# Taking layer 2's edge columns before the normalization instead of after it, and adding both with one operation

## The chip, the cores and the metric

The kernel runs on one core of a Trainium2 chip. The metric is the device time of one execution in microseconds (us), the median over the runs. The engines are named as in the profile: PE is TensorE's matmul, PEld its weight load, DVE is VectorE, ACT is ScalarE, POOL is GpSimd, SP is SyncE, which issues most DMAs. Each engine works through its own instructions in order.

## The reference

Input x is 16 images of 64 channels and 128x128 pixels, float32. Four layers follow one another, each x = x + f(gn(x)), where gn is a group normalization over 32 groups of two channels.

- Layer 0: f builds the 64x64 Gram matrix of an image's channels and multiplies the image by it, then by a 64x64 matrix.
- Layer 1: f is the sum of the absolute values of two fixed 3x3 derivative filters per channel.
- Layer 2: the first 16 channels are shifted one column to the left, the next 16 one column to the right (zeros come in), and a 3x3 convolution with 64 output channels and a bias follows.
- Layer 3: a 3x3 convolution with weights -1, 0, 1, a 1x1 convolution, a batch normalization over all images, a leaky ReLU and a clip.

## The kernel before

Everything works on 128 partitions: 64 channels times two halves (halves of the image or the two row parities). An image is cut into NS = 8 chunks. Four stages are pipelined over images and chunks: `Gram` (layer 0's matrix), `Front` (layers 0 and 1), `Layer2` and `Layer3` (up to the batch normalization's sums). What is left of layer 3 needs sums over all images; it is a last part that loads two tensors, combines them and stores the output.

**The order is written out by hand.** An outer loop goes over steps, each step over four quarters q = 0, 1, 2, 3. In a quarter, the stages are called in the order Layer3, Layer2, Front, then Gram, and within a stage the images in rising order. One image has its eight chunks i = 0 to 7 in eight successive steps, and stages run a few steps ahead (`first`) and behind (`last`): at the step in which image b-1 is at i = 7 in `Layer2`, image b is at i = -1. Additional calls named "first of 3", "last of 0" and "last of 3" put single operations at the front or the end of a quarter. The wrapper `InOrder` keeps each engine's instructions in the order in which the program makes them, so that this order is what every engine works through. Short chains of tiny operations for statistics (`coefficients`, `gram_chain`) advance by one link per quarter.

**Layer 2, chunk by chunk.** For chunk c of an image:

- `load(c)` is called at i = c-2, q = 1. SP issues 6 DMAs (12 for chunk 7) that bring layer 1's result, channels already shifted, into a tile `v2` of 9 rows of 128 and one more element at each end (128x1154); `whole` is all of the tile, `v` its 9x128 middle.
- At i = c-1, q = 1, ACT normalizes the whole tile in place (`v<-v,co` in the profile, 128x1154). Then POOL makes the edge columns: four `tensor_scalar_mul` of 64x8 each (`edges<-v,co`), one for each side and each half of the partitions. They pick the elements that the shift pushed over the edge out of the normalized tile, multiplied by 1/r (r is gn's factor) where the channel is a left-shifted or a right-shifted one, else by zero. After them, two more POOL operations (`v<-v,kc`, 128x9, "keep") set the columns that the shift has to leave zero.
- At the end of that step ("last of 3"), DVE takes the difference of row parities (`d<-v`) and `twin(1)` has POOL issue two DMAs that copy it to the other half (`qd<-d`). At i = c, q = 0, a second difference is taken, and `twin(0)` has POOL issue two more.
- At i = c, q = 2 and 3, PE multiplies, in shared (`one<-v,wi`) and own products (`two<-d,wi`, `two<-d,w`, `two<-qd,pk`), into PSUM tiles `one` and `two`. At the front of q = 3 ACT moves `one` to SBUF with the bias (`c<-one,co`). `one` has a single buffer, so layer 3's first product of the next chunk (`one<-v,w`) waits for this `c`.
- At i = c+1, q = 0, DVE adds the two edge columns to PSUM's `two` with two operations of 128x8 (`two<-two,edges`), then makes the result x3 with its row sum (`x<-two,c`, 128x1024).

**Around it.** DVE's order in a step is: layer 1's first two operations (`u<-xh`, `e<-xh`), the edge columns and `x<-two,c`, the difference `d<-v`, four operations of layer 1 (`u<-u`, `e<-e`, `u<-u`, `e<-e`), layer 3's `y<-two,c`, then more differences and layer 1's last operations. ACT's order is: layer 3's `c<-one,b_sb` and normalizations `v<-x,co`, layer 2's `v<-v,co`, a copy for Gram (`xw<-xr`), layer 1's two absolute values (`u<-u`, `e<-e`, which need DVE's second pair), a square `junk<-x`, normalizations `xh<-po`, layer 2's `c<-one,co`, and so on. Buffers that matter: `v2` has 3, `edges` 3, PSUM's `one` 1.

The coefficients of layer 2 are a tile of six columns (`co2`): r, -mean*r, 1/r, 1/r masked for left, 1/r masked for right, mean plus bias.

Of the kernel before, what the change touches and what calls it, by code (L numbers as in the profile page):

```python
# [10 lines left out]
F32 = mybir.dt.float32  # L11
AF = mybir.ActivationFunctionType
ALU = mybir.AluOpType
AX = mybir.AxisListType

B, C, H, W = 16, 64, 128, 128
P = 128
# [3 lines left out]
R = 8  # L21
NS = HH // R
# [86 lines left out]
def tile_kernel(ctx: ExitStack, tc: tile.TileContext, x, cw_h, w2_t, b2, wbin_t, w1_t, b1, gamma, beta, consts, out):  # L109
    nc = tc.nc  # L110
    pe, dve, act, sp, pool = (InOrder(tc, e) for e in (nc.tensor, nc.vector, nc.scalar, nc.sync, nc.gpsimd))
# [8 lines left out]
    def k(name):  # L120
        return kc[:, AT[name][0]:AT[name][1]]
# [14 lines left out]
    def flat(ap):  # L136
        return ap.rearrange("p j w -> p (j w)")
# [18 lines left out]
    stp = ctx.enter_context(tc.tile_pool(name="stp", bufs=2))  # L156
# [6 lines left out]
    def sv(name, n=1):  # L163
        return small.tile([P, n], F32, tag=name, name=name)
# [115 lines left out]
    def coefficients(st, put, back=None):  # L280

        s2 = sv("s2", 2)
        dve.tensor_reduce(s2, st, axis=AX.X, op=ALU.add)
        yield
        pm = sm(2)
        small_product(pm, k("gmean"), s2)
        yield
        co = sv("co", 2) if back is None else sv("co2", 6)
        me = sv("me", 2)
        r, mean = co[:, 0:1], me[:, 0:1]  # L290
        yield from rstd(pm, r, me, GN_EPS)
        dve.scalar_tensor_tensor(co[:, 1:2], mean, -1.0, r, op0=ALU.mult, op1=ALU.mult)
        if back is not None:

            dve.reciprocal(co[:, 2:3], r)
            dve.tensor_mul(co[:, 3:4], co[:, 2:3], k("left"))
            dve.tensor_mul(co[:, 4:5], co[:, 2:3], k("right"))
            dve.tensor_add(co[:, 5:6], mean, back)
        put(co)


# [125 lines left out]
    rows = []  # L427
# [103 lines left out]
    class Front:  # L531
# [138 lines left out]
        def store(self, i):  # L670
            d = planes(x2_d[self.b]).rearrange("(c s) j w -> c s j w", s=2)
            for h in range(2):
                for s in range(2):
                    j0 = (h * HH + i * R) // 2
                    sp.dma_start(
                        d[:, s, j0:j0 + R // 2, :],
                        self.x2[i][h * C:(h + 1) * C].rearrange("p (j s) w -> p s j w", s=2)[:, s],
                    )
# [68 lines left out]
    class Layer2:  # L747
# [7 lines left out]
        def load(self, i):  # L755
# [14 lines left out]
            self.v[i] = t[:, 1:N - 1].rearrange("p (j w) -> p j w", w=W)  # L770
            self.whole[i] = t

        def store(self, i):

            d, t = x3_d[self.b], tiles3[self.b][i]
            for s in range(2):
                v = pairs(d, 1)[:, i * R:(i + 1) * R, :].rearrange("c (n s) w -> c s n w", s=2)
                sp.dma_start(v[:, s], t[hi, s])
            for s in range(2):
                j = i * R + 1 + s  # L780
                m = CP if i + 1 < NS or s == 0 else CP - 1
                if j + 2 * m <= NP:
                    v = pairs(d, 0)[:, j:j + 2 * m, :].rearrange("c (n s) w -> c s n w", s=2)[:, 0]
                else:
                    v = pairs(d, 0)[:, j - 1:j - 1 + 2 * m, :].rearrange("c (n s) w -> c s n w", s=2)[:, 1]
                sp.dma_start(v, t[lo, s, 0:m])
            if i + 1 == NS:
                sp.dma_start(pairs(d, 0)[:, 0:1, :], t[lo, 1, CP - 1:CP])
# [24 lines left out]
        def at(self, i, q):  # L813
            b = self.b
            closing = i + 1 == NS
            m = CP - 1 if closing else CP
            if q == 0:
                if i == NS:
                    chains.append(coefficients(self.st, self.done))
                if 1 <= i:  # L820
                    two = self.p.pop(i - 1)[0]

                    e = self.edges.pop(i - 1).rearrange("p t (m n) -> p t n m", n=2)
                    for side, w in ((0, 0), (1, W - 1)):
                        dve.tensor_add(two[:, :, :, w], two[:, :, :, w], e[:, side])
                    x3 = ring.tile([P, 2, CP, W], F32, tag="x3", name=f"x3_{b}_{i - 1}", bufs=NS + 2)
                    tiles3[b].append(x3)
                    dve.scalar_tensor_tensor(
                        x3.rearrange("p s j w -> p s (j w)"), two.rearrange("p s j w -> p s (j w)"), 1.0,
                        self.c.unsqueeze(1).to_broadcast([P, 2, CP * W]),  # L830
                        op0=ALU.mult, op1=ALU.add, accum_out=self.st[:, 0, i - 1:i],
                    )
                if 0 <= i < NS:
                    difference("d2", 0, self.v[i], m)
                    self.twin(0)
            if q == 1:
                if i == 0:

                    self.wi = stp.tile([P, 2, 3, P], F32, tag="wi", name=f"wi_{b}", bufs=1)
                    for n, base in ((0, w2[:, 2]), (1, wm)):  # L840
                        dve.scalar_tensor_tensor(
                            self.wi[:, n].rearrange("p k o -> p (k o)"), k("I3"), self.co[:, 2:3],
                            base.rearrange("p k o -> p (k o)"), op0=ALU.mult, op1=ALU.add,
                        )
                if -1 <= i < NS - 1:
                    if i == -1:
                        self.co = coefs2.pop(b)
                    t, f = self.v[i + 1], self.whole.pop(i + 1)
                    act.activation(f, f, AF.Identity, bias=self.co[:, 1:2], scale=self.co[:, 0:1])


                    e = stp.tile([P, 2, R], F32, tag="edges", name=f"edges_{b}_{i + 1}", bufs=3)
                    for side, at in ((0, 0), (1, W + 1)):
                        for rows, j in ((lo, 1), (hi, 0)):
                            n = at + j * W
                            pool.tensor_scalar_mul(
                                e[rows, side], f[rows, n:n + (R - 1) * W + 1:W], self.co[rows, 3 + side:4 + side]
                            )
                    self.edges[i + 1] = e

                    pool.tensor_scalar_mul(t[:, :, 0], t[:, :, 0], k("keep0"))
                    pool.tensor_scalar_mul(t[:, :, W - 1], t[:, :, W - 1], k("keep1"))
                if i + 2 < NS:
                    self.load(i + 2)
            if q == 2:
                if 0 <= i < NS:
                    t = self.v[i]
                    one = ps_one.tile([P, CP, W], F32, tag="one", name=f"one2_{b}_{i}")
                    two = ps_two.tile([P, 2, CP, W], F32, tag="two", name=f"two2_{b}_{i}")
                    self.p[i] = two, one  # L870
                    shared(one, self.wi[:, 0], t, m)
                    if closing:
                        small_product(one[:, m, :], w0, t[:, R, :])

                    both = self.wi[:, 1]
                    own(two[:, 1], 1, TO_SLOTS, w2, "d2", m, both)
                    if closing:

                        p = two[:, 1, m:CP]
                        issue([taps(0, p, [both], [t[:, R:R + 1, :]]), taps(1, p, [both], [t[:, R - 1:R, :]])])  # L880
                if 1 <= i < NS:
                    self.square(i - 1)
                if 1 <= i:
                    self.store(i - 1)
            if q == 3:
                if 0 <= i < NS:
                    t = self.v.pop(i)
                    two, one = self.p[i]
                    both = self.wi[:, 1]
                    own(two[:, 0], 0, TO_SLOTS, w2, "d2", m, both)  # L890
                    if closing:
                        p, srcs = two[:, 0, m:CP], [t[:, R - 2:R - 1, :], t[:, R - 1:R, :]]
                        issue([taps(0, p, [w2[:, 0], both], srcs), taps(1, p, [both, w2[:, 1]], srcs)])
            if q == "first of 3" and 0 <= i < NS:
                self.c = ring.tile([P, CP * W], F32, tag="c2", name=f"c2_{b}_{i}", bufs=1)
                act.activation(self.c, flat(self.p[i][1]), AF.Identity, bias=self.co[:, 5:6])
            if q == "last of 0" and i == NS:
                self.square(i - 1)
            if q == "last of 3" and -1 <= i < NS - 1:
                difference("d2", 1, self.v[i + 1], CP if i + 2 < NS else CP - 1)  # L900
                self.twin(1)


    class Layer3:
# [266 lines left out]
```

## Time and profile before

| what | value |
|---|---|
| median of 3 runs | 2755.46 us (2754.84 to 2756.58) |
| the profiled execution | 2756.86 us; its span from the first to the last instruction is 2755.1 us |
| busy in the span: PE, PEld, DVE, ACT, POOL | 2159.6, 886.9, 2192.4, 2113.5, 943.2 us |
| busy in the eight steps 1214.71 to 1347.18 (132.47 us): PE, DVE, ACT, POOL | 129.80, 126.50, 121.90, 56.87 us |
| start-up, until the stages are all at work | about 0 to 420 us |
| all stages at work | about 420 to 2080 us |
| last images of layers 2 and 3, no Front | about 2080 to 2300 us |
| last part, bound by DMA at some 410 to 420 GB/s | about 2300 to 2755 us |

Every instruction of the wrapped engines is recorded at one line, L73, that of the wrapper. Rows are therefore told apart by their tiles, written "output<-inputs". In a timeline a row is: start in us, duration in us, engine, line, operation, tiles, sizes, count, and in brackets how long the engine stood idle before it and what released it. In the list of waits a row is: who waited, for whom, us in total, times, longest. Times of the stretches of one image are taken from image 8 (the first chunk's normalization of layer 2 starts at 1214.71 us), where the order has settled.

### The profile page before, as it was taken

The numbers are of one execution on the slowest core, as the hardware profiler recorded it, in microseconds if no ns is written. First come the engines' busy times: TensorE is split into PE (matmuls) and PEld (weight loads), VectorE is DVE, ScalarE is ACT, GpSimd is POOL, SyncE is SP. The second block draws the span as 40 slices with busy tenths as digits, with TensorE's granted clock in tenths as the row PEclk, the third lists the DMA queues.
The fourth block names the chain that finished last, engine by engine and source line by source line (L and its number), as shares of the span: only waits on it lengthen the run. The fifth ranks groups of instructions, "written<-read, shape, count | busy, mean of one in ns | idle before, by whom it ended". The sixth has DMA issues, their size and how long they took to land. (4 is left out here: it accounts for less than half of the span.)

```text
span 2755.1 us, 46091 instructions
## 1 busy us (share of the span) xinstructions
PE 2159.6 (78%) x14804; PEld 886.9 (32%) x14804; DVE 2192.4 (80%) x3623; ACT 2113.5 (77%) x3177; POOL 943.2 (34%) x1350
## 2 busy tenths in 40 slices
PE   6578799999999999999999999999999994000000
PEld 4233333434343434343434343333334641000000
DVE  4998899899999999999999999999996335333332
ACT  4766779998989898989898989899997667333332
POOL 2055444444444444444434444454544300000000
PEclk8689899999999999999999999999999997555555
DMA  8799779898888898888888887888887768999999
GB/s 206 200 229 233 196 183 249 214 244 220 235 224 233 215 240 224 234 227 224 230 228 226 223 203 192 208 207 206 216 207 192 219 191 297 419 420 420 420 420 384
DMA packets 693601, 685.96 MB, mean 249 GB/s; under 512 B 60096, under 2 KB 580448, under 8 KB 693360
## 3 DMA queue, kind: packets, MB, share of 16 engines
q1 hardware_dynamic: 668208, 613.83, 76.0%
q0 software_dynamic: 25152, 69.18, 9.9%
q8 instruction: 119, 1.95, 0.3%
q14 instruction: 122, 1.00, 0.1%
HBM read 346.23 MB, written 268.44 MB: 223 GB/s over the span
## 5 line engine op out<-in xcount | busy, mean ns | idle before, releaser
L73 PE MATMUL two<-d,w 128*64 128x508 f32 (+2 forms) x2560 | 837.5, 587 | 0.0
L73 PE MATMUL two<-d,wi 128*64 128x508 f32 (+3 forms) x1536 | 572.7, 578 | 0.0
L73 POOL DMA_DIRECT2D qd<-d x512 | 270.8, 531 | 851.5 <-issue 295.8
L73 PE MATMUL two<-qd,pk 128*64 128x512 f32 (+1 forms) x1024 | 518.3, 587 | 10.1 <-DMA qd<-d 8.8
L73 POOL TENSOR_SCALAR edges<-v,co 64x8 f32<-64x8 f32 x512 | 397.7, 777 | 287.4 <-ACT v L73 204.0
L73 DVE TENSOR_TENSOR d<-v 128x512 f32<-128x512 f32 (+1 forms) x512 | 346.5, 679 | 58.4 <-issue 29.7
L73 PE MATMUL one<-v,w 128*64 128x508 f32 (+2 forms) x1600 | 364.6, 580 | 30.1 <-ACT c L73 30.1
L73 PEld LDWEIGHTS two<-d,w 128*64 128x64 f32 x2560 | 265.8, 136 | 326.3 <-issue 289.8
L73 PE MATMUL one<-v,wi 128*64 128x508 f32 (+3 forms) x1536 | 360.6, 602 | 1.5 <-issue 1.4
L73 ACT COPY qd<-d 64x512 f32<-64x512 f32 x512 | 315.5, 616 | 18.6 <-DVE d L73 12.5
L73 DVE SCALAR_TENSOR_TENSOR e<-e 128x1032 f32<-128x1032 f32 (+1 forms) x256 | 313.2, 1223 | 0.0
L73 ACT ACTIVATE xh<-po,co 128x128 f32<-128x128 f32 (+1 forms) x480 | 274.9, 621 | 31.0 <-PE po L73 24.9
L73 POOL TENSOR_SCALAR v<-v,kc 128x9 f32<-128x9 f32 x256 | 246.7, 976 | 11.9
L73 ACT ACTIVATE u<-u 128x1024 f32<-128x1024 f32 x128 | 135.7, 1060 | 144.2 <-DVE u L73 144.2
L73 PEld LDWEIGHTS two<-d,wi 128*64 128x64 f32 x1536 | 177.5, 136 | 193.5 <-issue 179.2
L73 ACT ACTIVATE v<-x,co 128x512 f32<-128x512 f32 (+2 forms) x368 | 235.0, 705 | 0.0
L73 DVE SCALAR_TENSOR_TENSOR y<-two,c 128x1024 f32<-128x1024 f32 x128 | 156.0, 1219 | 94.0 <-ACT v L73 68.2
L73 PE MATMUL po<-x,abd 64*64 64x512 f32 (+1 forms) x1024 | 177.7, 641 | 43.9 <-ACT xh L73 41.6
L73 PEld LDWEIGHTS one<-v,w 128*64 128x64 f32 x1600 | 124.6, 136 | 227.9 <-issue 139.5
L73 PEld LDWEIGHTS two<-qd,pk 128*64 128x64 f32 x1024 | 136.0, 136 | 151.1 <-issue 101.9
L73 DVE SCALAR_TENSOR_TENSOR u<-xh 128x1170 f32<-128x1170 f32 x128 | 175.4, 1371 | 4.8 <-ACT xh L73 4.5
L73 PEld LDWEIGHTS one<-v,wi 128*64 128x64 f32 x1536 | 109.3, 139 | 195.9 <-issue 188.3
(165 smaller groups left out, 3321.0 us busy)
## 6 DMA issues: line engine op xcount, KB each, us to landing
x<-in_x SPq DMA_DIRECT2D x256, 256.0 KB, 4.6
x_d<-u SPq DMA_DIRECT2D x512, 128.0 KB, 4.0
y_d<-y SPq DMA_DIRECT2D x512, 128.0 KB, 3.8
x_d<-x SPq DMA_DIRECT2D x496, 128.0 KB, 2.8
xr<-in_x SPq DMA_DIRECT2D x120, 512.0 KB, 6.5
qd<-d POOLq DMA_DIRECT2D x256, 130.0 KB, 3.1
qd<-d POOLq DMA_DIRECT2D x256, 129.8 KB, 3.9
v<-x_d SPq DMA_DIRECT2D x448, 72.1 KB, 2.9
```

Of the source, the lines that this page charges most:

```text
L73: return self.tc.keep_in_program_order(call(*args, **kwargs))
```

## The change

The edge columns are taken from the tile as it was loaded, before the normalization: instead of (normalized value) times (masked 1/r), POOL computes (loaded value minus mean) times mask, one operation with two scalars per partition. This is done by a new function `sides(c)`. For chunk 0 it is called at i = -1, q = 0; for chunk c from 1 on at i = c-2, "last of 3", after `twin(1)`: two quarters ahead of the normalization, which stays where it was, at i = c-1, q = 1. The four POOL operations after the normalization are gone, so the two keep operations follow it directly. The normalization overwrites what `sides` reads, so it now comes after `sides` for the same chunk. On DVE, the two edge additions become one of 128 x 4 x 2 x 2 elements, and the coefficient chain has one operation fewer (five columns instead of six).

```diff
         if back is not None:
             dve.reciprocal(co[:, 2:3], r)
-            dve.tensor_mul(co[:, 3:4], co[:, 2:3], k("left"))
-            dve.tensor_mul(co[:, 4:5], co[:, 2:3], k("right"))
-            dve.tensor_add(co[:, 5:6], mean, back)
+            dve.tensor_copy(co[:, 3:4], mean)
+            dve.tensor_add(co[:, 4:5], mean, back)
...
+        def sides(self, i):
+            e = stp.tile([P, 2, R], F32, tag="edges", name=f"edges_{self.b}_{i}", bufs=3)
+            for side, at, which in ((0, 0, "left"), (1, W + 1, "right")):
+                for rows, j in ((lo, 1), (hi, 0)):
+                    n = at + j * W
+                    pool.tensor_scalar(
+                        e[rows, side], self.whole[i][rows, n:n + (R - 1) * W + 1:W], self.co[rows, 3:4],
+                        k(which)[rows], op0=ALU.subtract, op1=ALU.mult,
+                    )
+            self.edges[i] = e
...
-                    e = self.edges.pop(i - 1).rearrange("p t (m n) -> p t n m", n=2)
-                    for side, w in ((0, 0), (1, W - 1)):
-                        dve.tensor_add(two[:, :, :, w], two[:, :, :, w], e[:, side])
+                    e = self.edges.pop(i - 1).rearrange("p t (m n) -> p n m t", n=2)
+                    ends = two[:, :, :, 0:W:W - 1]
+                    dve.tensor_add(ends, ends, e)
...
                 if 0 <= i < NS:
                     difference("d2", 0, self.v[i], m)
                     self.twin(0)
+            if q == 0 and i == -1:
+                self.co = coefs2.pop(b)
+                self.sides(0)
             if q == 1:
...
                 if -1 <= i < NS - 1:
-                    if i == -1:
-                        self.co = coefs2.pop(b)
                     t, f = self.v[i + 1], self.whole.pop(i + 1)
                     act.activation(f, f, AF.Identity, bias=self.co[:, 1:2], scale=self.co[:, 0:1])
-                    e = stp.tile([P, 2, R], F32, tag="edges", name=f"edges_{b}_{i + 1}", bufs=3)
-                    for side, at in ((0, 0), (1, W + 1)):
-                        for rows, j in ((lo, 1), (hi, 0)):
-                            n = at + j * W
-                            pool.tensor_scalar_mul(
-                                e[rows, side], f[rows, n:n + (R - 1) * W + 1:W], self.co[rows, 3 + side:4 + side]
-                            )
-                    self.edges[i + 1] = e
                     pool.tensor_scalar_mul(t[:, :, 0], t[:, :, 0], k("keep0"))
                     pool.tensor_scalar_mul(t[:, :, W - 1], t[:, :, W - 1], k("keep1"))
...
             if q == "last of 3" and -1 <= i < NS - 1:
                 difference("d2", 1, self.v[i + 1], CP if i + 2 < NS else CP - 1)
                 self.twin(1)
+                if i + 2 < NS:
+                    self.sides(i + 2)
```

The bias of `c<-one,co` is read from column 4 instead of column 5.

More of the change, by code (lines that the diff above doesn't have):

```diff
@@ L287, in coefficients @@
         yield
-        co = sv("co", 2) if back is None else sv("co2", 6)
+        co = sv("co", 2) if back is None else sv("co2", 5)
         me = sv("me", 2)
@@ L895, in at @@
                 self.c = ring.tile([P, CP * W], F32, tag="c2", name=f"c2_{b}_{i}", bufs=1)
-                act.activation(self.c, flat(self.p[i][1]), AF.Identity, bias=self.co[:, 5:6])
+                act.activation(self.c, flat(self.p[i][1]), AF.Identity, bias=self.co[:, 4:5])
             if q == "last of 0" and i == NS:
```

## The prediction

> **What bounds the kernel now.** I read the page first, then the waits of the long stretch with all stages at work, the busy time step by step for one image (image 8), and last the timelines of the engines at that image's first chunk. The page's busy shares (PE 78%, DVE 80%, ACT 77%) don't decide. Table by step, from one layer-2 normalization to the next (us; busy PE, PEld, DVE, ACT, POOL; clock; DMA), its first four rows and its sum:
>
> ```profile
> 1214.71:1233.87 19.16, 19.16 (x138) 10.21 (x134) 17.28 (x25) 17.63 (x29) 9.46 (x12) 1.00 0.95 261
> 1233.87:1250.54 16.67, 14.98 (x74) 4.58 (x72) 16.29 (x30) 14.25 (x23) 7.02 (x10) 1.00 0.88 231
> 1250.54:1266.61 16.07, 15.09 (x76) 4.60 (x74) 15.92 (x21) 15.98 (x26) 7.32 (x12) 1.00 0.92 252
> 1266.61:1281.57 14.96, 14.96 (x80) 4.59 (x76) 14.60 (x20) 14.87 (x25) 7.08 (x11) 1.00 0.84 223
> ...
> sum 132.47, PE 129.80 PEld 51.75 DVE 126.50 ACT 121.90 POOL 56.87; mean PE 16.23 PEld 6.47 DVE 15.81 ACT 15.24 POOL 7.11
> ```
>
> PE has no gap in six of the eight steps; its only idle time is in the second and third, 2.67 us per image. So **PE sets the pace**, DVE and ACT have very little to spare, and a gain on DVE counts only where PE waits. For what does it wait (420 to 2080 us)?
>
> ```profile
> PE one L73 <- ACT c L73: 29.9, 26, 1.9
> PE two L73 <- DMA qd<-d: 4.3, 5, 1.5
> ```
>
> It waits for ACT to empty the single buffer of `one`. The chain behind that wait is in the timelines of ACT and DVE: ACT works without a pause from `e<-e` at 1219.60 to `junk<-x`, which ends at 1231.2; DVE waits 1.73 us for it and then works through to `nv`; ACT waits for that, makes `c`, and PE goes on at 1241.49. So **an ACT delay at the first chunk of an image, once over ACT's idle time there, reaches PE**. How much idle time is there, and what does POOL do at that moment? ACT, POOL, and DVE beside it:
>
> ```profile
> 1214.71 1.34 ACT L73 ACTIVATE v<-v,co 128x1154 f32<-128x1154 f32 x1
> 1215.95 1.19 ACT L73 COPY xw<-xr 128x1024 f32<-128x1024 f32 x1
> 1218.46 1.06 ACT L73 ACTIVATE u<-u 128x1024 f32<-128x1024 f32 x1 [1.32 <-DVE u L73]
> 1219.60 1.06 ACT L73 ACTIVATE e<-e 128x1024 f32<-128x1024 f32 x1
> ```
> ```profile
> 1215.56 1.03 POOL L73 DMA_DIRECT2D qd<-d  x2 [6.06 <-issue]
> 1216.61 3.90 POOL L73 TENSOR_SCALAR edges<-v,co 64x8 f32<-64x8 f32 x4
> 1220.61 2.64 POOL L73 TENSOR_SCALAR v<-v,kc 128x9 f32<-128x9 f32 x2
> ```
> ```profile
> 1214.44 0.56 DVE L73 TENSOR_TENSOR d<-v 128x384 f32<-128x384 f32 x1
> ...
> 1218.34 1.22 DVE L73 SCALAR_TENSOR_TENSOR e<-e 128x1024 f32<-128x1024 f32 x1
> 1219.48 1.22 DVE L73 SCALAR_TENSOR_TENSOR y<-two,c 128x1024 f32<-128x1024 f32 x1
> ```
>
> ACT has 1.32 us to spare. POOL issues `twin(0)` of the previous image's last chunk at 1215.56, right after DVE's `d<-v`, and its four edge operations take 3.90 us, to 1220.51. Undisturbed they are far shorter (median 318 ns each).
>
> [...] at 1268.06 an edge operation beside `y<-two,c` (one input in PSUM) takes 318 ns; at 1216.61, under layer 1's two-input operations, the first of the four takes 1.91 us and the second 1.16. [...] so I give the subtract-multiply form the present form's time. No row shows it. [...]
>
> **The change, part by part.**
>
> 1. *One edge addition fewer, 128 times.* The two run from 1212.81 to 1213.19, the second starting some 0.2 us after the first. Saved: 0.2 us of DVE per chunk [...]. In the steps in which PE is busy throughout it is worth nothing by itself. It counts only where it lies in the chain to PE's wait, ahead of `e<-e` at 1219.6: one addition per image, since DVE resynchronizes with PE at 1207.55 (a wait of 1.28 us) and with ACT at 1231.35. If the one addition cost as much as two: 0.
> 2. *Coefficient chain.* Two 1-element products become one copy: some 0.07 us per image, on the same stretch. Together DVE is 0.27 us earlier per boundary.
> 3. *Four POOL operations less between normalization and keep.* DVE waits for the keeps 19 times, 7.4 us in all up to 2080 us (3.9 us of it before 420 us). These waits go, but DVE isn't the bound after 420 us; before it I count a gain of 0 to 4 us.
> 4. *`sides(c)` for chunks 1 to 7*, queued on POOL behind `twin(1)` and ahead of `twin(0)`. It also waits for the load. For chunk 2 of image 8, `twin(1)` ends at 1244.4 and the load has landed; DVE's two-input `e<-xh` ends at 1246.8; then come the addition and `x<-two,c`, both with one input in PSUM, to 1248.4. Four operations of 0.31 plus 0.07 us between them make 1.5 us, so they fit, before `twin(0)` at 1249.56 and ACT's normalization at 1250.54. Cost 0; if the window is missed, `twin(0)` is late, and with it PE's `two<-qd,pk` (a wait that already occurs, 4.3 us in all): 0 to 8 us over the run. In image 0, chunk 1 has no such window: 0 to 5 us, set against part 3.
> 5. *`sides(0)`*, called at q = 0 after the previous image's call, so **on POOL behind that image's last `twin(0)`**, and ahead of ACT's `v<-v,co` by the new dependency. `twin(0)` can't go before DVE's `d<-v`, and ends at 1216.6. `sides(0)` then stands exactly where the edge row above stands, beside the same DVE operations, and takes the same 3.90 us: it ends at 1220.51 less 0.27 (parts 1, 2), 5.5 us after ACT would have started the normalization. Before, those 3.9 us had only the keeps behind them. Now ACT waits, and behind its `v<-v,co` stand `xw`, `u<-u`, `e<-e`, `junk<-x`, `xh`, `c<-one,co`. New start of `u<-u`: 5.55 + 2.3 (normalization and copy) = 7.85 after the old start, before 3.75; `e<-e` loses 0.1 less. **4.0 us later.** `c<-one,co` (old end 1223.29) passes PE's `one<-v,w` (1224.34), so PE loses 3.0 us there and the last 1.0 us at the next chunk, where its wait grows from 1.7 to 2.7.
>
> The same sum at the other boundaries, with each one's own rows (edge end after the normalization's start; ACT's idle time):
>
> | image | edges end | idle before u | delay |
> |---|---|---|---|
> | 4 to 10 | 5.8 | 1.3 | 7 x 4.0 = 28.0 |
> | 2, 3 | 4.5, 4.8 | 0, 0.3 | 4.2 + 4.0 = 8.2 |
> | 11, 12 | 6.3, 5.8 | 2.9, 2.4 | 3.0 + 3.0 = 6.0 |
> | 13, 14 | 4.8 | 1.4 | 2 x 3.0 = 6.0 |
> | 1 | 8.7 | 4.4 | 3.9, of which I take 3.0 |
> | 0, 15 | | over 1.6 | 0 |
>
> Images 11 to 14 have no copy between, hence 1.24 instead of 2.3. In image 1 PE has idle time of its own. Sum: **51 us**. Nothing gives it back: after the third chunk PE is gapless, and the last part starts when the sums are ready. The profiled execution (2756.9, span 2755.1) would become 2808; the median, 1.4 us below it, 2806.5.
>
> **Rivals.**
>
> - *A. `sides(0)` passes quickly*, at the undisturbed 0.38 us each: done 1.6 us after `twin(0)`. Then the delay is 1.7 us at images 4 to 10, 1.4 and 2.0 at 2 and 3, some 0.8 at 11 to 14, 1 at image 1: 20 us, 2775. Against it: the row of 3.90 us in the same place.
> - *B. It takes longer*: with two scalars the fourth operation misses the gap of `y<-two,c` and waits behind the next `d<-v` (0.7 us), 14 times, 10 us; with some late `twin(0)` of part 4, up to 2824.
> - *C. Faster.* POOL has idle time from `twin(1)` (done at 1209.5) to 1215.5, and the load is there 2.4 us before the normalization. If `sides(0)` ran in that gap, only parts 1 to 3 are left: 14 x 0.27 = 3.8 plus 0 to 4 us, 2749. It decides where the four operations end before ACT's 1.3 us are used up. Against it: the images are called in rising order, and POOL keeps program order.
> - *D. The merged addition saves nothing*: 0.2 x 14 = 3 us more than the main case.
>
> **How the numbers follow.** Main case, with D and small misses, 0.75 (2795 to 2820); A or something between 0.11; B 0.08; C 0.06. The range 2780 to 2826 takes in the main case, most of B and half of A. A difference of 0.2%, 5.5 us, is about what can be told from none. C gives less than that as often as more: faster 0.04, same 0.03, slower 0.93.
>
> **What would show it.** In the new profile, ACT's `v<-v,co` of each first chunk waits some 5.5 us for POOL's `edges` (new in the list of waits, some 60 to 75 us in all); the four `edges` come right behind `qd<-d` and still take 3.9 us; `u<-u` no longer waits for DVE there; PE's wait for `c` grows from 29.9 to some 75 us. Chunks 1 to 7 show no such wait, `two<-two,edges` falls to 128 of some 180 ns, DVE's wait for `v` is gone. I am wrong if ACT doesn't wait at the first chunks, or waits while PE's idle time stays.

## The result, and the profile after

| what | before | after |
|---|---|---|
| median, measured side by side | 2755.78 us (4 runs) | 2840.36 us (4 runs, 2838.46 to 2841.65) |
| ratio after to before | | 1.0309 (95% interval 1.0296 to 1.0322) |
| profiled execution, its span | 2756.86, 2755.1 us | 2841.14, 2839.4 us |

The change costs 84.6 us. Forecast were 51, and at most 70 within the range: the direction and the place were right, the size was not.

The table by step for the same image 8, from one normalization of layer 2 to the next (us; busy PE, PEld, DVE, ACT, POOL; clock; DMA):

```profile
1266.74:1284.22 17.48, 14.08 (x91) 6.04 (x91) 10.58 (x16) 17.35 (x27) 5.82 (x10) 0.90 0.69 179
1284.22:1300.85 16.63, 15.40 (x76) 4.70 (x74) 16.28 (x29) 14.24 (x24) 8.72 (x10) 1.00 0.78 204
1300.85:1318.32 17.47, 16.53 (x82) 5.04 (x80) 17.36 (x22) 16.07 (x26) 9.24 (x10) 1.00 0.92 263
1318.32:1333.28 14.96, 13.41 (x70) 4.55 (x68) 14.04 (x18) 14.88 (x23) 8.91 (x13) 1.00 0.87 198
...
1380.98:1405.76 24.78, 24.78 (x215) 10.48 (x213) 22.39 (x46) 15.70 (x27) 9.45 (x11) 1.00 0.98 258
sum 139.02, PE 131.90 PEld 51.13 DVE 124.99 ACT 121.79 POOL 63.01; mean PE 16.49 PEld 6.39 DVE 15.62 ACT 15.22 POOL 7.88
```

The eight steps take 139.02 instead of 132.47 us: 6.55 more per image. A wait of ACT ahead of its normalization counts in the step that ends there, so the last row (24.78) holds the wait of the next image's first chunk. PE is now idle in four steps instead of two: 3.40 us in the first, and 1.55 in the fourth, where it had no gap before. DVE's and ACT's own work has not grown; POOL's has, by 6 us per image, and PE's by 2.10 us (131.90 against 129.80). Most of the last comes from the clock: in the kernel before, the clock granted to PE is 1.00 throughout the stretch with all stages at work; here it is 0.50 for 3.4 us, from 1274.7 us on, soon after PE's idle 3.40 us, and twelve products of `one<-v,w` that take 2.78 us at the next chunk take 4.39.

The list of waits of the stretch with all stages at work, now 420 to 2165 us (who waited, for whom, us in total, times, longest):

```profile
ACT v L73 <- POOL edges L73: 106.0, 28, 6.9
...
PE one L73 <- ACT c L73: 63.9, 34, 4.6
...
PE two L73 <- DMA qd<-d: 25.9, 14, 2.7
```

The first row is new, and PE's wait for `c` has doubled from 29.9 us; both were forecast. The third was 4.3 us and should have stayed there. So there are two losses.

**The first loss: the first chunk.** POOL, ACT, DVE and PE at image 8's first chunk:

```profile
1260.68 1.03 POOL L73 DMA_DIRECT2D qd<-d  x2 [5.64 <-issue]
1261.75 4.96 POOL L73 TENSOR_SCALAR edges<-v,co,kc 64x8 f32<-64x8 f32 x4
1268.19 0.62 POOL L73 TENSOR_SCALAR v<-v,kc 128x9 f32<-128x9 f32 x2 [1.48 <-ACT v L73]
```
```profile
1266.74 1.35 ACT L73 ACTIVATE v<-v,co 128x1154 f32<-128x1154 f32 x1 [6.39 <-POOL edges L73]
1268.00 1.14 ACT L73 COPY xw<-xr 128x1024 f32<-128x1024 f32 x1
1269.03 1.05 ACT L73 ACTIVATE u<-u 128x1024 f32<-128x1024 f32 x1
...
1272.97 0.68 ACT L73 ACTIVATE c<-one,co 128x512 f32<-128x512 f32 x1
```
```profile
1263.46 1.22 DVE L73 SCALAR_TENSOR_TENSOR e<-e 128x1024 f32<-128x1024 f32 x1
1264.60 1.22 DVE L73 SCALAR_TENSOR_TENSOR y<-two,c 128x1024 f32<-128x1024 f32 x1
...
1265.74 0.69 DVE L73 TENSOR_TENSOR d<-v 128x512 f32<-128x512 f32 x1
1270.11 1.29 DVE L73 SCALAR_TENSOR_TENSOR u<-xh,co,u 128x1024 f32<-128x1024 f32 x1 [3.68 <-ACT u L73]
```
```profile
1273.70 4.39 PE L73 MATMUL one<-v,w 128*64 128x512 f32 x12 [3.40 <-ACT c L73]
```

Up to PE's first wait the forecast chain is there link by link: `edges` directly behind `qd<-d`, ACT's normalization behind `edges`, `u<-u` without a wait, `c` late, PE idle for `c`. Only the size differs: the four operations take 4.96 us instead of the 3.90 that I carried over from the old row. One by one in the trace they take 3056, 405, 393 and 865 ns (before: 1912, 1156, 303, 311). The first ends at 1264.80, 0.2 us after `y<-two,c`, with one input in PSUM, has started. The second and third fit beside that one. The fourth begins 0.1 us after the next two-input operation, `d<-v` (1265.74), and ends only after it. Only behind that wait a link was off: PE's wait for `c` at the second chunk was to grow from 1.7 to 2.7 us and fell to 1.23, since PE had spent 1.6 us more on the slow products. Idle time and slow products at these two chunks are 4.5 us more than before; forecast were 4.0.

**The second loss: the fourth chunk.** The same image, POOL, DVE, ACT and PE at chunk 3, at which nothing was forecast:

```profile
1311.63 0.20 POOL L628 MEMSET xh<- 64x130 f32 x1 [1.21 <-DVE two L73]
1311.93 6.36 POOL L73 TENSOR_SCALAR edges<-v,co,kc 64x8 f32<-64x8 f32 x4
1318.23 1.10 POOL L73 DMA_DIRECT2D qd<-d  x2
```
```profile
1311.40 0.17 DVE L73 TENSOR_TENSOR two<-two,edges 128x16 f32<-128x16 f32 x1
1311.68 1.23 DVE L73 SCALAR_TENSOR_TENSOR x<-two,c 128x1024 f32<-128x1024 f32 x1
...
1312.83 0.69 DVE L73 TENSOR_TENSOR d<-v 128x512 f32<-128x512 f32 x1
```
```profile
1318.32 1.35 ACT L73 ACTIVATE v<-v,co 128x1154 f32<-128x1154 f32 x1 [1.31 <-POOL edges L73]
```
```profile
1322.74 0.61 PE L73 MATMUL two<-qd,pk 128*64 128x512 f32 x1 [1.54 <-DMA qd<-d]
```

The window between `e<-xh` and `d<-v` opens at 1311.40. POOL, done with `twin(1)` at 1310.42, first stands idle for 1.21 us until it can zero a halo row (`MEMSET`, line 628, which is outside the order by hand), and zeroes it for 0.20 us; the edge operations are queued behind. Two of them fit; the third starts at 1312.89, 0.06 us after `d<-v`, and takes 3034 ns, the fourth 2281. That delays the normalization by 1.31 us, and `twin(0)`, queued behind, goes out at 1318.23; its transfer is what PE then waits for.

The additions are as forecast. From the operations on the tiles (shortest, median and longest in ns), after:

```profile
L73 DVE TENSOR_TENSOR two<-two,edges x128: 167/175/250, 185.1 to 2308.5; 128x16 f32<-128x16 f32 x128
```

### The profile page after: what moved, and what is told of

The parts are those of the page before. It is cut to its first block, busy times and chain, and to the rows that moved or that the text cites. A ratio compares the mean times of both kernels' runs of the same rounds, so it can differ in the third digit from the quotient of the medians.

```text
span 2839.4 us, 45821 instructions
## 1 busy us (share of the span) xinstructions
PE 2184.8 (77%) x14804; PEld 881.9 (31%) x14804; DVE 2168.5 (76%) x3479; ACT 2110.9 (74%) x3177; POOL 1021.1 (36%) x1350
## 5 line engine op out<-in xcount | busy, mean ns | idle before, releaser
L73 POOL DMA_DIRECT2D qd<-d x512 | 279.0, 546 | 841.4 <-DVE d L73 448.1
L73 POOL TENSOR_SCALAR edges<-v,co,kc 64x8 f32<-64x8 f32 x512 | 511.3, 999 | 85.6 <-DMA v<-x_d 48.2
L73 PE MATMUL one<-v,w 128*64 128x508 f32 (+2 forms) x1600 | 383.1, 608 | 64.4 <-ACT c L73 64.2
L73 POOL TENSOR_SCALAR v<-v,kc 128x9 f32<-128x9 f32 x256 | 205.1, 812 | 230.1 <-ACT v L73 229.8
L73 ACT ACTIVATE v<-v,co 128x1154 f32<-128x1154 f32 x128 | 172.2, 1345 | 139.2 <-POOL edges L73 124.2
L73 DVE SCALAR_TENSOR_TENSOR u<-xh,co,u 128x1024 f32<-128x1024 f32 x128 | 163.9, 1280 | 69.3 <-ACT u L73 69.2
```

Of the source, the lines that this page charges most:

```text
L73: return self.tc.keep_in_program_order(call(*args, **kwargs))
```

## The experiments

My theory after the result: everything comes from one number. The edge operation with two scalars per partition is longer than the one with a single scalar, so it costs 1.07 us more at each first chunk and misses the window at chunk 3. The rivals: the place of the operations costs, whatever their length (the tile just loaded, other queues); or the loss at chunk 3 is a follow-on of that at the first chunk. The ratios are to the kernel before. Each median stands against runs of the kernel before on the same chip (2755.4 to 2755.5 us).

**Which chunks: only 1 to 7 early.** Chunk 0's edges are made after the normalization with the old formula (two more coefficient columns), the others early.

```diff
-                self.sides(0)
...
+                    if i == -1:
+                        self.late(0, f)
```

> Chunk 0's edge columns are made after its normalization, as in the kernel before; chunks 1 to 7 and the merged addition as in the changed kernel. Theory (the loss is ACT waiting at each image's first chunk for the edge operations that stand behind the previous image's last copy): the wait of 5.4 to 6.9 us at first chunks is gone, 14 boundaries of some 4.9 us come back, 2770 to 2780 us; what remains over 2755 is the wait at the chunk with the memset (some 1.4 us per image). Rival (the early operations of chunks 1 to 7 carry most of it, by making POOL's copies late, PE's wait for them having grown from 4 to 31 us): 2805 to 2825 us.

2773.76 us (four runs, 2768.67 to 2783.53), ratio 1.0071 (1.0049 to 1.0092). The waits at the first chunks are gone, PE's wait for `c` is 23.8 us over the whole run; PE's wait for `qd<-d` (30.9 us) and the loss at chunk 3 (1.40 us at image 8) are all there. So the second loss does not follow from the first: 18 us.

**Which chunks: only chunk 0 early.** The reverse.

```diff
+                    if i >= 0:
+                        self.late(i + 1, f)
...
-                if i + 2 < NS:
-                    self.sides(i + 2)
```

> The other half: only chunk 0's edge columns are made early, chunks 1 to 7 after their normalization. Theory: 2815 to 2822 us, ACT waits for POOL at first chunks only. Rival: 2770 to 2790 us.

2812.42 us, ratio 1.0206 (1.0189 to 1.0223): 57 us, 3 us below the range of the theory. PE's wait for `qd<-d` is back at 3.1 us in the whole run, chunk 3 loses nothing. The two halves make 75 of the 84.6 us. The other 10 would be lost only when both are there, but the three intervals together are nearly as wide (some 8 us).

**Where chunk 0 stands in POOL's queue.** `sides(0)` is called at the front of q = 0, ahead of the previous image's `twin(0)`.

```diff
-            if q == 0 and i == -1:
+            if q == "first of 0" and i == -1:
...
-                if q == 3:
-                    run(Layer2, b, step - starts[1][1] - NS * b, "first of 3")
+                if q in (0, 3):
+                    run(Layer2, b, step - starts[1][1] - NS * b, f"first of {q}")
```

> The changed kernel with chunk 0's early edge operations called at the front of the quarter, so that they stand on POOL ahead of the previous image's last copy instead of behind it. Theory (the place in POOL's queue is the cause): ACT's wait at first chunks falls under 1 us, 2770 to 2785 us, as without early operations there. Rival (the operations are too slow in any place, since the load lands only 2.4 us ahead and DVE's two-input operations follow): the wait stays over 3 us, 2810 us or more.

2777.15 us, ratio 1.0078 (1.0063 to 1.0093). The first loss goes with the order alone: image 8's operations end 0.03 us before the normalization would start anyway, and ACT does not wait. In all, ACT's waits at first chunks fall from 87.4 to 12.0 us, 7.0 of them in image 0. This is Rival C's order. The queue behind `twin(0)` is thus shown as the cause of the first loss; the second stays.

**The length of the operation: one scalar.** The changed kernel, but each edge operation only subtracts the mean; the mask is left out.

```diff
-                    pool.tensor_scalar(
+                    pool.tensor_scalar_sub(
                         e[rows, side], self.whole[i][rows, n:n + (R - 1) * W + 1:W], self.co[rows, 3:4],
-                        k(which)[rows], op0=ALU.subtract, op1=ALU.mult,
                     )
```

> The changed kernel with one operation and one scalar per element in the early edge operations (mean subtracted, the mask left out, so that the edge columns of channels that aren't shifted are computed differently). Theory (the second scalar makes each operation some 400 ns instead of 318, so that the four miss gaps between DVE's two-input operations; that is what the forecast missed): operations of 310 to 320 ns, the first chunk's four take 3.9 us instead of 5.0, the wait at the chunk with the memset goes, 2800 to 2812 us. Rival (the size of the operation doesn't matter[...]): operations of 318 ns or not, 2832 to 2841 us.

2794.56 us, ratio 1.0142 (1.0127 to 1.0157). Nothing is moved, and 46 of the 84.6 us are gone, more than the theory's range had. POOL and ACT at image 8's first chunk, with one scalar:

```profile
1236.34 3.89 POOL L73 TENSOR_SCALAR edges<-v,co 64x8 f32<-64x8 f32 x4
```
```profile
1240.27 1.35 ACT L73 ACTIVATE v<-v,co 128x1154 f32<-128x1154 f32 x1 [5.30 <-POOL edges L73]
```

This is the picture that I had forecast (3.90 us, a wait of 5.5), and the loss at chunk 3 is gone too (0.00 us at image 8, PE's wait for `qd<-d` 4.5 us in the whole run). So the place fixes that ACT waits, and the length of one POOL operation fixes how long. That length also decides whether chunk 3 joins, together with two things tried below: the zeroing and the width of the window.

**What makes it long: the second operation or the second scalar?** Subtract and multiply as in the changed kernel, but multiplied by the number 0.25 instead of the mask's column.

```diff
-                        k(which)[rows], op0=ALU.subtract, op1=ALU.mult,
+                        0.25, op0=ALU.subtract, op1=ALU.mult,
```

> The changed kernel with the mask column replaced by the fixed number 0.25 in the edge operations: subtract and multiply, but one scalar per partition. Theory 1, the second operation costs: still 392 to 407 ns each and some 2840 us. Theory 2, the second scalar read per partition costs: about 301 to 318 ns and some 2795 us, as with the mean alone (2794.6).

2797.38 us in one run: as with the mean alone. The rows of the edge tiles (number of operations, shortest/median/longest in ns), in the kernel before, after, with the mean alone, and with the number:

```profile
L73 POOL TENSOR_SCALAR edges<-v,co x512: 299/318/4456, 153.2 to 2203.6; 64x8 f32<-64x8 f32 x171
```
```profile
L73 POOL TENSOR_SCALAR edges<-v,co,kc x512: 392/406/3514, 151.5 to 2282.9; 64x8 f32<-64x8 f32 x171
```
```profile
L73 POOL TENSOR_SCALAR edges<-v,co x512: 301/313/2417, 149.4 to 2234.9; 64x8 f32<-64x8 f32 x171
```
```profile
L73 POOL TENSOR_SCALAR edges<-v,co x512: 316/330/2437, 150.4 to 2238.2; 64x8 f32<-64x8 f32 x171
```

Medians: 318, 406, 313, 330 ns. The second operation adds 17 ns; taking the second scalar from a column, one per partition, instead of a fixed number adds 76.

Under DVE the difference is larger. I counted, in the traces, the edge operations that start during a DVE operation with two SBUF inputs and have three more such operations behind it without a pause. In the changed kernel all 29 of them end 0.19 us after the third of these has started. With the mean alone, 29 of 31 end 0.17 to 0.18 us after the second has started, and with the number 29 of 31 again (0.18 to 0.20). So there the second column costs one DVE operation more, some 1.1 us, and not 76 ns. The first operation at the first chunk follows the same count: with one scalar it takes 1909 ns and ends 0.18 us after the second has started, with two it takes 3056 and ends 0.20 us after the third, `y<-two,c`.

**The two scalars in the old place.** The edges after the normalization, as before, but with two scalar columns (times 1/r, times the mask).

```diff
-                            pool.tensor_scalar_mul(
-                                e[rows, side], f[rows, n:n + (R - 1) * W + 1:W], self.co[rows, 3 + side:4 + side]
+                            pool.tensor_scalar(
+                                e[rows, side], f[rows, n:n + (R - 1) * W + 1:W], self.co[rows, 2:3],
+                                k("left" if side == 0 else "right")[rows], op0=ALU.mult, op1=ALU.mult,
                             )
```

> The kernel before with the merged addition, and its edge operations in their old place, after the normalization, but as one operation with two scalars per partition (times 1/r, times the mask). Theory 1, the second scalar makes the operation longer: the shortest ones take about 390 to 410 ns where they took 299 to 318, and the time stays within 0.2% of the one with the merged addition alone, since only the keeps wait behind them. Theory 2, it is the place (the tile just loaded instead of the tile just normalized) that makes them longer: 300 to 320 ns.

The expectation names the merged addition by mistake: the kernel that ran has the two additions of the kernel before, and is compared with that. 2764.36 us, ratio 1.0030 (1.0018 to 1.0041). The tile's row:

```profile
L73 POOL TENSOR_SCALAR edges<-v,co,kc x512: 336/360/4486, 153.1 to 2208.5; 64x8 f32<-64x8 f32 x171
```

The second scalar, together with the second operation, makes the operation longer in the old place too, but by 42 ns, not the 90 that I expected. Two things differ from the changed kernel, the operation (two multiplications here, subtract and multiply there) and the place; which of them makes 360 of 406 was not separated. With one scalar the two places differ by 5 ns (318 and 313). "Only the keeps wait behind them" was wrong as well: DVE's wait for POOL's keeps grew from 7.4 to 17.4 us, and the time by 9 us.

**The zeroing at chunk 3.** The two zeroings take their place in the order by hand.

```diff
-                nc.gpsimd.memset(self.chunk(0)[lo, 0, :], 0.0)
+                pool.memset(self.chunk(0)[lo, 0, :], 0.0)
...
-                    nc.gpsimd.memset(self.chunk(NS - 1)[hi, R + 1, :], 0.0)
+                    pool.memset(self.chunk(NS - 1)[hi, R + 1, :], 0.0)
```

> The changed kernel with one thing moved: the two zeroings of layer 1's halo rows on POOL keep the place in the order in which the program makes them (in the changed kernel the one of chunk 7 ran at 1311.63 us, in front of chunk 3's edge operations). Theory 1, the zeroing tips chunk 3 out of its window: its four edge operations are over before layer 2's normalization, ACT's wait at chunk 3 (1.31 us at image 8, 2.9 us at images 11 to 14) is gone, and with it 1.4 us per image for images 2 to 10 and 2.8 us for 11 to 14: some 20 us less, 2817 to 2824. Theory 2, the operations are too long for the window with or without the zeroing: unchanged, 2837 to 2843, the third operation still takes 3 us.

2817.41 us, ratio 1.0224 (1.0208 to 1.0239): 23 us back, by moving an operation of 0.20 us for which POOL had waited 1.21. POOL at image 8's chunk 3, now without the zeroing in front:

```profile
1296.34 1.09 POOL L73 DMA_DIRECT2D qd<-d  x2 [5.23 <-DVE d L73]
1297.47 4.31 POOL L73 TENSOR_SCALAR edges<-v,co,kc 64x8 f32<-64x8 f32 x4
1301.73 1.10 POOL L73 DMA_DIRECT2D qd<-d  x2
```

The first operation now starts right behind `twin(1)`, while `e<-xh` still runs, and is over 0.3 us after it (1286 ns); two follow in the window, and only the fourth misses it (1984 ns). The edges end 2.1 us ahead of the normalization.

**The merged addition undone.** The changed kernel with the two additions of before.

```diff
-                    e = self.edges.pop(i - 1).rearrange("p t (m n) -> p n m t", n=2)
-                    ends = two[:, :, :, 0:W:W - 1]
-                    dve.tensor_add(ends, ends, e)
+                    e = self.edges.pop(i - 1).rearrange("p t (m n) -> p t n m", n=2)
+                    for side, w in ((0, 0), (1, W - 1)):
+                        dve.tensor_add(two[:, :, :, w], two[:, :, :, w], e[:, side])
```

> The changed kernel with the two edge additions of the kernel before instead of the merged one. It measures what part 1 gives inside the changed kernel. Theory 1, the saving counts at the boundaries and in images 11 to 14, as it did in the kernel before (11 us): 2846 to 2852. Theory 2, with ACT late at every boundary DVE has time to spare and the saving counts for nothing: 2839 to 2843.

2835.05 us, ratio 1.0287 (1.0270 to 1.0304). Both theories missed: in the changed kernel the merged addition does not gain, nor count for nothing; it costs 5 us. POOL and DVE at image 8's chunk 3, with two additions:

```profile
1306.45 0.20 POOL L628 MEMSET xh<- 64x130 f32 x1 [1.21 <-DVE two L73]
1306.74 5.33 POOL L73 TENSOR_SCALAR edges<-v,co,kc 64x8 f32<-64x8 f32 x4
```
```profile
1306.22 0.37 DVE L73 TENSOR_TENSOR two<-two,edges 128x8 f32<-128x8 f32 x2
1306.70 1.23 DVE L73 SCALAR_TENSOR_TENSOR x<-two,c 128x1024 f32<-128x1024 f32 x1
...
1307.85 0.69 DVE L73 TENSOR_TENSOR d<-v 128x512 f32<-128x512 f32 x1
```

From the first addition to `d<-v` are 1.63 us here and 1.43 with the merged one. In the longer window the third operation starts 0.14 us before `d<-v` and takes 931 ns instead of 3034; ACT waits 0.49 instead of 1.31 us. At chunk 3 of every image from 2 to 10 this wait is 0.4 to 0.7 us here and 1.3 with the merged one. The change has shortened the very window that it then needed.

**The merged addition alone.** The kernel before with that edit only.

```diff
-                    e = self.edges.pop(i - 1).rearrange("p t (m n) -> p t n m", n=2)
-                    for side, w in ((0, 0), (1, W - 1)):
-                        dve.tensor_add(two[:, :, :, w], two[:, :, :, w], e[:, side])
+                    e = self.edges.pop(i - 1).rearrange("p t (m n) -> p n m t", n=2)
+                    ends = two[:, :, :, 0:W:W - 1]
+                    dve.tensor_add(ends, ends, e)
```

> The kernel before with only the merged addition of the two edge columns on DVE; the edges are made where they were, after the normalization. Forecast of part 1: 0.2 us less at each of 14 boundaries, 2751 to 2754 us. Rival (a chunk's 0.2 us counts nowhere): 2755 to 2756. Second rival (it counts in every chunk): 128 times 0.2, 2730.

2744.45 us, ratio 0.9958 (0.9946 to 0.9971): 11 us faster than before, four times the 2.8 us that my 14 boundaries gave at 0.2 each, and outside all three forecasts. No version measured here was faster. The PE wait of image 13's second chunk, in the kernel before and with the merged addition:

```profile
1889.30 2.78 PE L73 MATMUL one<-v,w 128*64 128x512 f32 x12 [1.43 <-ACT c L73]
```
```profile
1876.52 2.78 PE L73 MATMUL one<-v,w 128*64 128x512 f32 x12 [0.20 <-ACT c L73]
```

So at this image DVE's 0.2 us of every chunk do count, though PE shows no gap in six of the eight steps: DVE gets ahead by 0.2 us in each of most chunks, and PE's wait at the second chunk takes it in, 1.2 us there and as much at image 14. At image 12 that wait stays (1.91 and 1.89 us).

**Both orders mended.** `sides(0)` ahead of `twin(0)`, and the zeroings in order.

```diff
-            if q == 0 and i == -1:
+            if q == "first of 0" and i == -1:
...
-                nc.gpsimd.memset(self.chunk(0)[lo, 0, :], 0.0)
+                pool.memset(self.chunk(0)[lo, 0, :], 0.0)
...
```

> The changed kernel with both: the edges of chunk 0 are called in front of the previous image's transfer (as in the version that measured 2777.2 us), and the two zeroings keep their place on POOL. Theory 1, the two waits are all of the loss in the steady stretch: what is left is image 0 and gains of parts 1 to 3, 2752 to 2762 us. Theory 2, the zeroing is not the cause of chunk 3's wait: 2774 to 2780.

2757.45 us, ratio 1.0005 (0.9996 to 1.0013). Theory 1 holds: with both waits out of the way the change costs nothing against before. It still loses 13 us against the merged addition alone.

**Both orders mended, and one scalar.** On top of these edits the mask is left out.

```diff
-                    pool.tensor_scalar(
+                    pool.tensor_scalar_sub(
...
-                        k(which)[rows], op0=ALU.subtract, op1=ALU.mult,
```

> The version with both mends (chunk 0's edges called in front of the previous image's transfer, the zeroings in their place on POOL; 2757.5 us), but each edge operation only subtracts the mean: one operation, one scalar; the mask is left out. The kernel before with the merged addition alone took 2744.5 us. Theory 1, what is left of the 13 us between the two is the length of the early operations in the windows of image 0 and of single chunks: 2741 to 2749. Theory 2, the place itself costs (POOL's transfers later, layer 2's loads waited for in image 0): 2752 to 2758.

2744.96 us, ratio 0.9964 (0.9953 to 0.9975). The 13 us go with the operation's length; where in the run they lie is not shown, since the profiled execution was the slowest of its seven (2753.11 us). With short operations and the right order the kernel is as fast as with the merged addition alone, within some 5 us: the move, with the shorter coefficient chain and the ordered zeroings, neither gains nor costs more than that, and the one gain shown is that of the merged addition.

**Where in the run.** How far each profiled execution lags behind that of before (us), taken from the starts of the normalization of the third chunk of images 2, 10 and 14, and from the end of the execution. The forecast row sums my table in the same way.

| kernel | until image 2 | images 3 to 10 | 11 to 14 | rest | sum |
|---|---|---|---|---|---|
| forecast | 7.2 | 32.0 | 12.0 | 0 | 51.2 |
| after | 8.2 | 55.6 | 19.4 | 1.1 | 84.3 |
| one scalar | 1.1 | 30.8 | 6.0 | -0.6 | 37.3 |
| zeroings in order | 8.5 | 38.3 | 14.1 | -1.0 | 59.9 |
| merged addition alone | -7.6 | -2.1 | -4.5 | -1.0 | -15.2 |

(The profiled execution of the last one lies 2.7 us below its median, that of before 1.4 us above its own, hence 15.2 instead of 11.) With operations of the length that I assumed, the forecast's 32.0 for images 3 to 10 meets 30.8. Until image 2 and in 11 to 14 that kernel stays 6 us below the forecast each. The merged addition alone gains 7.6 and 4.5 us in these two stretches, which I had not counted and which may be the reason. So the 51 us were too many for the operations that I had assumed, and the two errors partly cancel.

## Why the prediction was wrong in size

**The step that failed is one term**: "I give the subtract-multiply form the present form's time. No row shows it." I took 318 ns, it is 406, and where DVE works on two SBUF inputs one whole DVE operation more (1909 to 3056 ns). With operations as short as I assumed, 46 of the 84.6 us are gone. Rival B did allow for a longer operation at the boundary (0.7 us), but part 4 passed it at no cost. That the second operation and the second column would add nothing was my estimate, and no trace had shown it. Measured are 17 ns for the operation (313 to 330) and 76 for the column (330 to 406).

By the prediction's parts, at image 8 where not said otherwise:

1. *One addition.* The size of the operation was right: 175 ns, forecast some 180, which was my estimate (each of the two takes 174 before). Its worth was not: "in the steps in which PE is busy throughout it is worth nothing by itself" holds for images 3 to 10 (2.1 us in eight images, 0.26 each; forecast 0.2), and fails for 11 to 14 (1.1 per image on average) and the start (7.6 us until image 2; for what reason is not shown). In the changed kernel its sign turns.
2. *Coefficient chain*: not tried by itself. In the traces it is shorter by more than the 0.07 us forecast: from the last reciprocal `co<-co` to `u<-xh` are 0.41 us before and 0.19 after, where the first product started 0.19 us after that reciprocal, and the copy, which doesn't use it, starts 0.07 us after it.
3. *Four POOL operations less before the keeps.* DVE's wait for the keeps has left the list, as forecast. A gain at the start does not show: the lag until image 2 is 8.2 us.
4. *Chunks 1 to 7, "cost 0".* Wrong: 18 us with only these early. I had checked the window at chunk 2 with 4 x 0.31 + 0.07 between = 1.5 us. At 0.40 and 0.08 between, four take 1.84 us. The window had shrunk as well: the one that I read from the old trace held two additions, with one it is 1.43, and at chunk 3 a zeroing goes first, 0.20 us and a wait of 1.21 ahead of it. It stands in the old trace too, at 1261.54; I had looked at chunk 2 only. I had named what is late next if the window is missed (`twin(0)`, then `two<-qd,pk`), and so it came, but with 0 to 8 us as its price, where a miss costs whole DVE operations: 3.03 and 2.28 us.
5. *Chunk 0.* Place, order, releaser and the links up to PE's first wait right. 4.96 instead of 3.90 us for the four, ACT's wait 6.39 instead of 5.5. Net per boundary 4.8 us; forecast 4.0; with one scalar 3.7. The 1.1 us between the first and the last are the 4.96 less 3.89.

**Rival B** had the mechanism of the fourth operation (behind `d<-v`, 0.7 us at each boundary) and came out at 865 ns; I gave it 0.08 and added late `twin(0)` only as "some". It was nearer than my main case. It missed the first operation (3.06 instead of 1.91 + 0.07 + 1.16, nearly even in sum). **Rival A** is excluded by the row of 4.96. **Rival C**, the order with `sides(0)` in POOL's gap, is what the mended order shows; it was excluded for the right reason, the program's order. Its 2749 was not reached with that order alone (2777.15), as the loss at chunk 3 stays. **Rival D**: the one addition takes 175 ns where two took 174 each, so it does save its time. But inside the changed kernel it is worth less than nothing, and there Rival D was nearer than the main case.

PE's wait for `c` rose to 63.9 us against 75 forecast, ACT's wait for edges to 106 against 60 to 75: 79 at first chunks and 27 at others, 22 of these at chunk 3. "Chunks 1 to 7 show no such wait" was the sign by which the failure could be seen, and it was.

What stays open: why two multiplications with two columns take 360 ns and subtract-multiply with two columns 406; what the start (until image 2) owes to which part; and whether the half clock behind PE's longer pauses costs anything beyond the waits.

## What to carry to other kernels

When a row's duration is carried over to a changed instruction, list what differs in its form, operand by operand (here one more scalar column), and work the sum out a second time with a longer one; if the operation has to fit a window, ask what one miss costs, not what the operation costs. The small POOL operations here were priced by windows between DVE's two-input operations (at chunk 3 two inside the window took 0.39 and 0.40 us, the third, 0.06 us too late, 3.03): count what opens, shortens or fills each window, and whether the same change does so. And split a change into its edits before judging it: the one that here looked like a detail was worth 11 us alone, and the rest broke even at best in what was tried.

## What the hardware showed that I had not expected

- A second scalar column costs a POOL operation of 64x8 elements that subtracts and multiplies 76 ns (330 to 406); the second arithmetic operation only 17 (313 to 330). Two multiplications with two columns take 360, so the 76 are not a price for every operation.
- A POOL operation that starts under a two-input DVE operation can stay in flight through several of them: at chunk 3, one that starts 0.06 us after `d<-v` takes 3.03 us for 0.40 us of work, and one that starts 0.14 us before it takes 0.93. The counts above say how many: with two scalar columns it ended behind the start of the third DVE operation that followed (29 of 29), with one behind that of the second (29 of 31; in the kernel before 9 of 13, the others at the first, third or fifth). For two multiplications with two columns it was the second in 34 of 43 cases and the third in 8. Why the number follows the columns is not shown.
- Removing work from an engine can cost time where another engine used that moment: the second addition, 0.2 us with an input in PSUM, widened a window for POOL (1.63 against 1.43 us), and the changed kernel is 5 us faster with it (2835.05 against 2840.36).
- In the changed kernel the clock granted to PE fell to 0.50 twelve times between 420 and 2165 us, for 3.4 or 6.8 us, each time during a pause of PE of 2.0 us or more or within 1.02 us after it, though not at each such pause. In the kernel before, whose longest pause between 420 and 2080 us is 1.91 us, it never did there. That the pause is the reason is read from the times alone.
